# Attention through centers: projections of the next group in pieces, one copy on another engine, the first group in another order, and weight sums pinned later

## The chip, the cores and the metric

The kernel runs on one core of a Trainium2 chip. The metric is device time in microseconds, lower is better: 3571.76 us is the median of three runs before the change (3570.47 to 3575.51). The engines are called as in the profile: PE (TensorE matmul) and PEld (its weight loads), DVE (VectorE), ACT (ScalarE), POOL (GpSimd) and SP (SyncE, which issues most DMAs).

## What is computed

A decoder of four layers; each has an attention part, a cross-attention part and a feed-forward part, each added to `x` (16 sequences of 128 tokens, 256 wide, float32). The part that changes is the attention of layer 1, with 16 heads of width 16 and 64 centers for each head:

```python
def _affinity(t, centers, inv_two_sig2, amplitudes):
    t2 = jnp.sum(t * t, axis=-1, keepdims=True)
    c2 = jnp.sum(centers * centers, axis=-1)[None, :, None, :]
    tc = jnp.einsum('bhnd,hkd->bhnk', t, centers)
    d2 = jnp.maximum(t2 + c2 - 2.0 * tc, 0.0)
    return amplitudes[None, :, None, :] * jnp.exp(-d2 * inv_two_sig2[None, :, None, :])
...
q = split_heads(x @ W_q)
kk = split_heads(x @ W_k)
v = split_heads(x @ W_v)
q_aff = _affinity(q, centers, inv_two_sig2, amplitudes)
k_aff = _affinity(kk, centers, inv_two_sig2, amplitudes)
v_agg = jnp.einsum('bhnk,bhnd->bhkd', k_aff, v)
k_sum = jnp.sum(k_aff, axis=2)
num = jnp.einsum('bhnk,bhkd->bhnd', q_aff, v_agg)
den = jnp.einsum('bhnk,bhk->bhn', q_aff, k_sum) + EPS
out = num / den[..., None]
```

The output is projected with `W_o`. The cross-attention of layer 1 follows; its feed-forward part rescales its weights by the mean of their absolute values (`jnp.mean(jnp.abs(w))`), and the sums for that are computed during the cross-attention.

## The kernel before

The tokens are held in four groups (`x[g]`, 4 tiles of 128 tokens each). A scheduler places the recorded instructions on the engines. An instruction recorded with `keep_in_program_order` (the helpers `pinned`, L257, and `pinned_transpose`, L260) keeps its place among the others recorded so; one recorded with `mm` (L168) or `transpose_group` (L185), and all work on DVE, ACT and POOL, is put where the scheduler likes. PSUM has two sets of buffers: `b1`, four of one bank, and `b2`, two of two banks.

`l1_attn` (L843) loads its weights, scales the centers by the inverse widths, and makes two things of `c2`, the scaled squared lengths of the centers: `c2b` (in rows, for the keys) and `nc2` (through `c2col`, in a column, for the queries).

- `prologue(g)` (L891) is all of a group's projections at once: layernorm, the transposed rows `hT` (PE `tr`, one half copied out by DVE and the other by ACT, `evac`, L108), then `kT` and its squares, `qT` and its squares, and `v` of four tiles, copied by DVE and ACT in turn, beside two POOL memsets each.
- `queries(s, p)` (L916) makes the affinities `qa` of two tiles: 32 small products `yq`, eight exponentials on ACT (L935), and a clamp at 1 by two POOL instructions (L939).
- `keys(s, t)` (L942) does so for the keys of one tile: `yk`, two exponentials `ka` (L968), and the clamp on DVE (L969). A `yk` or a `yq` takes both `b2` buffers.
- `combine(...)` (L972) is a generator in six steps: `agg` and its scaling `vs` (DVE, L982); the transposes `aggT` and their copy `va` (ACT, L988); `num` and its copies `oT` (ACT, L1001); `o16t` and the division (DVE, `normalize`); `ctr` and its copy `cT` (DVE, L1013); the output projection `proj`, added to `x` (L222).

The loop at L1029 runs over the 16 tiles `n` and three iterations more. An iteration makes the keys of tile `n`, begins tile `n-1`, and takes steps of the tiles before. Odd iterations also make the queries of the next two tiles. At the end of the third iteration of each group stands the whole `prologue` of the next.

`xattn64` (L1047) is the cross-attention. It calls `beside[m]` at the end of its unit `m`; for layer 1 these come from `l1_ffn_begin` (L1225). Its `absolute(i)` (L1239) at units 10, 11 and 12 sums a weight matrix: one reduction over 2048 columns (L1241) and one over 16 (L1244), neither pinned.

Of the kernel before, what the change touches and what calls it, by code (L numbers as in the profile page):

```python
# [9 lines left out]
F = mybir.dt.float32  # L10
BF = mybir.dt.bfloat16
U32 = mybir.dt.uint32
AF = mybir.ActivationFunctionType
ALU = mybir.AluOpType
AX = mybir.AxisListType
PSUM = bass.MemoryType.PSUM

P = 128
# [4 lines left out]
NG = 4  # L23
GB = B // NG
GT = GB * P
# [5 lines left out]
class Decoder:  # L31
# [811 lines left out]
    def l1_attn(self):  # L843
# [6 lines left out]
        nc = self.nc  # L850
        wq, wk_, wv, wo = self.load4(["L1_attn_W_q", "L1_attn_W_k", "L1_attn_W_v", "L1_attn_W_o"])
# [5 lines left out]
        S = lambda t: slice(t * P, (t + 1) * P)  # L857
        R = lambda j: slice(32 * j, 32 * j + 32)
        with self.tc.tile_pool(name="l1a", bufs=1) as wk:
            c2b = wk.tile([P, 2, 4, P], F, tag="c2b", name="c2b")  # L860
            nc2 = wk.tile([P, 8], F, tag="nc2", name="nc2")
# [11 lines left out]
            c2 = self.hp.tile([P, 1024], F, tag="h", name="c2", bufs=2)  # L873
# [1 line left out]
            nc.vector.tensor_tensor(c2, cbf, cbf, ALU.mult)  # L875
            nc.vector.tensor_tensor(c2, c2, obf, ALU.mult)
            nc.vector.scalar_tensor_tensor(cbf, cbf, -2.0, obf, ALU.mult, ALU.mult)
            for half in range(2):
                ps = self.b1("c2b")
                self.mm(ps, [(self.ones, c2[:, half * 512 : (half + 1) * 512])])  # L880
                self.evac(c2b[:, half].rearrange("p r n -> p (r n)"), ps)
            ps = self.b1("c2col")[:, 0:8]
            for i in range(8):
                self.mm(ps[:, i : i + 1], [(c2[:, i * P : (i + 1) * P], self.ones[:, 0:1])])
            nc.vector.tensor_scalar(nc2, ps, -1.0, None, ALU.mult)

            for half in range(2):
                v = ob[:, half, :].rearrange("p (h k) -> p h k", h=8)
                nc.vector.tensor_tensor(v, v, self.hmask.unsqueeze(2).to_broadcast([P, 8, 64]), ALU.mult)

            def prologue(g):  # L891
                hT = self.hidden_T(self.layernorm(g))
                res = []
                for name, w in (("kT", wk_), ("qT", wq)):
                    if name == "kT":
                        dst, d2 = (wk.tile([P, 2, GT], F, tag=n, name=n, bufs=2) for n in ("kT", "kT2"))
                    else:
                        dst, d2 = (self.hp.tile([P, 2, GT], F, tag="hT", name=n, bufs=5) for n in ("qT", "qT2"))
                    for half in range(2):
                        ps = self.b1(name)  # L900
                        self.mm(ps, [(w[:, k, half * P : (half + 1) * P], hT[:, k, :]) for k in range(2)])
                        nc.vector.tensor_copy(dst[:, half, :], ps)
                        nc.scalar.activation(d2[:, half, :], dst[:, half, :], AF.Square)
                    res += [dst, d2]
                v = []
                for t in range(GB):
                    vt = wk.tile([P, 16, 32], F, tag="v32", name="v32", bufs=6)
                    nc.gpsimd.memset(vt[:, :, 16:32], 0.0)
                    nc.gpsimd.memset(vt[:, :, 16:17], 1.0)
                    ps = self.b1("v")[:, 0:DM]  # L910
                    self.mm(ps, [(hT[:, k, S(t)], wv[:, k, :]) for k in range(2)])
                    self.evac(vt[:, :, 0:16], ps.rearrange("p (h d) -> p h d", h=16))
                    v.append(vt)
                return res, v

            def queries(s, p):  # L916

                qT, qT2 = s[0][2:]
                cols = slice(p * 256, p * 256 + 256)
                tiles = [self.b2("yq").rearrange("p (r h n) -> p r h n", r=2, h=2) for _ in range(2)]  # L920
                for half in range(2):
                    for k, (w, q) in enumerate(((cb, qT), (ob, qT2))):
                        for r in range(4):
                            self.pinned(
                                tiles[r // 2][:, r % 2, half],
                                w[R(r), half, S(r)],
                                q[R(r), half, cols],
                                start=half == 0 and k == 0,
                                stop=half == 1 and k == 1,
                            )  # L930
                qa = wk.tile([P, 8, 256], F, tag="qa", name="qa", bufs=2)
                for r in range(4):
                    for half in range(2):
                        i = 4 * half + r
                        nc.scalar.activation(  # L935
                            qa[:, i, :], tiles[r // 2][:, r % 2, half], AF.Exp, bias=nc2[:, i : i + 1], scale=-1.0
                        )
                for i in range(0, 8, 4):
                    nc.gpsimd.tensor_scalar(qa[:, i : i + 4, :], qa[:, i : i + 4, :], 1.0, None, ALU.min)  # L939
                return qa  # L940

            def keys(s, t):  # L942

                kT, kT2 = s[0][:2]
                tiles = [self.b2("yk").rearrange("p (r n) -> p r n", r=2) for _ in range(2)]
                for r in range(4):
                    o = slice(32 * r, 32 * r + 1)
# [4 lines left out]
                        start=True,  # L952
                        stop=False,
# [18 lines left out]
            def combine(g, t, v, ka, qa):  # L972
# [12 lines left out]
                for m in range(2):  # L985
                    self.pinned_transpose(ps[:, S(m)], vs[:, S(m)])
                va = wk.tile([P, 2, 4, 32], F, tag="va", name="va", bufs=2)
                nc.scalar.copy(va.rearrange("p m j d -> p (m j d)"), ps)  # L988
                yield
                tiles = [self.b1("num")[:, 0:256] for _ in range(2)]  # L990
                cols = slice((t % 2) * P, (t % 2) * P + P)
# [26 lines left out]
                self.add_x(g, t, ps)  # L1018
                yield

            state = {0: prologue(0)}
            qas = {0: queries(state[0], 0)}
            kas, parts = {}, {}

            def part(n):
                if n in parts:
                    next(parts[n])

            for n in range(B + 3):  # L1029
                g, t = divmod(n, GB)  # L1030
                if n < B:
                    kas[n] = keys(state[g], t)
                part(n - 3)
                k = n - 1
                if 0 <= k < B:
                    parts[k] = combine(k // GB, k % GB, state[k // GB][1][k % GB], kas.pop(k), qas[k // 2])
                    part(k)
                if n % 2 and n + 1 < B:
                    qas[(n + 1) // 2] = queries(state[(n + 1) // GB], (n + 1) // 2 % 2)
                part(n - 2)  # L1040
                part(n - 1)
                part(n - 3)
                part(n - 1)
                if t == GB - 2 and g + 1 < NG:
                    state[g + 1] = prologue(g + 1)

    def xattn64(self, H, names, bias, tag, begin=None):  # L1047

# [176 lines left out]
    def l1_ffn_begin(self):  # L1225


        nc = self.nc
# [9 lines left out]

        def absolute(i):  # L1239
            p16 = self.small([P, 16], "p16")  # L1240
            nc.vector.tensor_reduce(  # L1241
                p16, flats[i].rearrange("p (a n) -> p a n", a=16), AX.X, ALU.add, apply_absolute_value=True
            )
            nc.vector.tensor_reduce(part[:, i : i + 1], p16, AX.X, ALU.add)  # L1244

# [1388 lines left out]
```

## Time and profile before

| | |
|---|---|
| median of three runs | 3571.76 us |
| the profiled execution, its own time | 3571.38 us |
| its span, first to last instruction | 3569.7 us |
| mean granted clock of TensorE over the span | 0.965 |
| the stage: last `down` of the part before, on PE | begins 1027.84 us |
| the stage: first product of its own, `c2b` | 1031.30 us |
| the stage: first product of the next part, `kT` at L1076 | 1219.11 us |
| va copies, L988 on ACT, within the stage | 16, mean 395 ns |
| DVE copies of the same shape out of PSUM, L1013 | 16, mean 419 ns |
| queries' clamp, L939 on POOL | 16, mean 2810 ns |
| keys' clamp, half as wide, L969 on DVE | 32, mean 489 ns |

The profile is one execution. A group of instructions is named by line, engine and operation, then what it writes and reads (`num<-qa,va`), its shape and how many there are. In brackets stands how long the engine had been idle before and what released it. In the tables of stretches, a row has the length of the stretch, busy time of PE, PEld, DVE, ACT and POOL with the number of instructions, the clock granted to TensorE as a share of full speed, the share of the DMA engines and their GB/s. The matmuls of the small forms (32 rows or 32 columns of the array) run beside each other, so that their durations overlap.

### The profile page before, as it was taken

How to read it: one execution, taken by the hardware profiler on the slowest of the kernel's cores; microseconds unless marked ns; L12 is line 12 of the kernel's file. 1: busy time of each engine (PE TensorE's matmuls, PEld its weight loads, DVE VectorE, ACT ScalarE, POOL GpSimd, SP SyncE). 2: the span in 40 equal slices, each digit the busy share in tenths (PEclk: the TensorE clock that was granted, in tenths of full speed). 3: DMA queues.
4: the chain of work that ended last, by engine and by line, in shares of the span. 5: the costliest groups of instructions: out<-in, count | busy, mean ns of one | idle time of the engine just before them, and what ended most of it. 6: DMA issues, size and time to landing. Idle time of an engine off the chain costs nothing.

```text
span 3569.7 us, 51436 instructions
## 1 busy us (share of the span) xinstructions
PE 3297.9 (92%) x20930; PEld 1787.4 (50%) x20947; DVE 2106.1 (59%) x4185; ACT 1426.3 (40%) x1924; POOL 424.5 (12%) x605
## 2 busy tenths in 40 slices
PE   7999999999998899998999997388999999999999
PEld 4666555555566566664555565252222222225656
DVE  5556444444544544568777544326999999953440
ACT  2357111111124322238555322024677777783221
POOL 5420000000013211110000210114000000002100
PEclk9999999999999999999999999697999999999989
DMA  2000000000110100010100000564202020000000
GB/s 78 1 23 15 18 18 23 18 18 23 36 38 2 38 1 1 1 43 8 46 1 13 2 1 1 182 201 131 36 12 32 12 32 11 11 1 26 1 8 18
DMA packets 90500, 105.46 MB, mean 30 GB/s; under 512 B 11380, under 2 KB 72694, under 8 KB 90006
## 3 DMA queue, kind: packets, MB, share of 16 engines
q1 hardware_dynamic: 79672, 89.71, 9.7%
q0 software_dynamic: 4224, 6.43, 0.6%
q10 hardware_dynamic: 6368, 6.03, 0.5%
q8 instruction: 165, 2.70, 0.3%
q14 instruction: 71, 0.58, 0.1%
HBM read 85.53 MB, written 16.60 MB: 29 GB/s over the span
## 4 chain that ended last, share of the span: by engine, by line
PE 79%; DVE 10%; ACT 5%; issue 3%; DMA 2%; POOL 1%; SPq 0%; POOLq 0%; ACTq 0%; DVEq 0%
PE acc L2166 7%; PE down L257 6%; PE gate L257 6%; PE up L257 6%; PE proj L257 6%; PE st L2166 5%; PE one L2166 4%; PE qT L168 4%; PE st L257 4%; PE o L257 2%; PE h L257 2%; DVE mx L2312 2%; PE rb L257 2%; PE fc L168 2%; PE pr L168 2%
## 5 line engine op out<-in xcount | busy, mean ns | idle before, releaser
L2312 DVE TENSOR_REDUCE mx<-one 128x1 f32<-128x512 f32 x1024 | 658.3, 686 | 55.6 <-PE one L2166 46.3
L2449 ACT ACTIVATE e<-st 128x1024 f32<-128x1024 f32 x512 | 497.0, 1021 | 207.2 <-PE st L2166 206.1
L803 ACT ACTIVATE gs<-gate,cols 128x512 f32<-128x512 f32 x132 | 90.7, 687 | 551.1 <-PE gate L257 544.1
L2166 PE MATMUL acc<-e,v 128*32 128x512 f32 x2048 | 284.7, 609 | 0.9 <-ACT e L2449 0.9
L817 DVE SCALAR_TENSOR_TENSOR x<-down,w_all,x 128x256 f32<-128x256 f32 x512 | 212.3, 477 | 110.4 <-PE down L257 110.2
L2166 PE MATMUL st<-qp,kp 113*128 113x512 bf16 x1024 | 271.6, 386 | 4.4 <-DMA qp<-shifts 2.1
L257 PE MATMUL down<-expert,gs 128*128 128x256 f32 x1056 | 249.5, 380 | 2.2 <-DVE gs L804 2.2
L257 PE MATMUL gate<-hT,expert 128*128 128x512 f32 x528 | 248.6, 593 | 0.2 <-ACT hT L712 0.2
L257 PE MATMUL up<-hT,expert 128*128 128x512 f32 x528 | 248.2, 593 | 0.0
L257 PEld LDWEIGHTS down<-expert,gs 128*128 128x128 f32 x1056 | 201.0, 190 | 85.2 <-issue 61.4
L804 DVE SCALAR_TENSOR_TENSOR gs<-up,cols,gs 128x512 f32<-128x512 f32 x132 | 98.9, 750 | 228.7 <-PE up L257 227.8
L2166 PE MATMUL one<-kp,qp 16*128 16x512 bf16 x1024 | 210.9, 395 | 3.7 <-DVE mx L2312 2.4
L2166 PEld LDWEIGHTS <-qp 16*128 16x128 bf16 x1024 | 49.0, 91 | 325.8 <-issue 320.5
L257 PEld LDWEIGHTS up<-hT,expert 128*128 128x128 f32 x528 | 100.5, 190 | 126.1 <-issue 126.1
L2166 PEld LDWEIGHTS <-kp 113*128 113x128 bf16 x1024 | 79.0, 98 | 141.5 <-issue 81.3
L1176 ACT COPY rb<-rb 128x512 f32<-128x512 f32 x64 | 37.4, 585 | 257.5 <-PE rb L257 257.5
L1178 DVE TENSOR_TENSOR cT<-o,rb 128x512 f32<-128x512 f32 x64 | 44.2, 691 | 155.3 <-ACT rb L1176 155.3
L257 PEld LDWEIGHTS gate<-hT,expert 128*128 128x128 f32 x528 | 99.8, 190 | 70.1 <-issue 63.4
L168 PE MATMUL qT<-hT,L_xattn_Wq 128*128 128x512 f32 x256 | 114.1, 599 | 6.7 <-DVE hT L112 4.5
L257 PE MATMUL o<-e,v 128*32 128x128 f32 (+1 forms) x2048 | 104.6, 277 | 12.6 <-DVE nm L294 11.8
L1485 DVE SCALAR_TENSOR_TENSOR xs<-xBC,cols,xs 128x508 f32<-128x508 f32 x144 | 106.0, 741 | 12.3 <-ACT xs L1481 9.0
L257 PEld LDWEIGHTS o<-e,v 128*32 128x32 f32 (+1 forms) x2048 | 80.9, 123 | 28.4 <-POOL e L335 12.3
(536 smaller groups left out, 5393.1 us busy)
## 6 DMA issues: line engine op xcount, KB each, us to landing
W<-in_L_ffn_W_dram SPq DMA_DIRECT2D x46, 512.0 KB, 5.2
expert<-in_L_ffn_Wg_dram SPq DMA_DIRECT2D x32, 128.0 KB, 2.2
expert<-in_L_ffn_Wu_dram SPq DMA_DIRECT2D x32, 128.0 KB, 2.6
expert<-in_L_ffn_Wd_dram SPq DMA_DIRECT2D x32, 128.0 KB, 2.5
parts<-parts SPq DMA_DIRECT2D x16, 256.0 KB, 2.5
qp<-parts SPq DMA_DIRECT2D x28, 128.0 KB, 3.8
kp<-parts SPq DMA_DIRECT2D x12, 256.0 KB, 8.5
hs<-zero SPq DMA_DIRECT2D x23, 128.0 KB, 1.8
```

Source lines behind the costliest of these rows:

```text
L168: self.nc.tensor.matmul(out, lhsT, rhs, start=i == 0, stop=i == n - 1 and bias is None)
L257: self.tc.keep_in_program_order(self.nc.tensor.matmul(*a, **k))
L803: nc.scalar.activation(gs, pg, AF.Silu, bias=bg)
L804: nc.vector.scalar_tensor_tensor(gs, pu, bu, gs, ALU.add, ALU.mult)
L817: nc.vector.scalar_tensor_tensor(xt, pd[:, t, :], w_all[:, o : o + 1], xt, ALU.mult, ALU.add)
L1176: nc.scalar.copy(rb, ps)
L1178: nc.vector.tensor_tensor(cT, po, rb, ALU.mult)
L1485: stt = lambda *a: pin(nc.vector.scalar_tensor_tensor(*a))
L2166: self.tc.keep_in_program_order(nc.tensor.matmul(*a, **k))
L2312: nc.vector.tensor_reduce(mx[:, t, kc, i : i + 1], pair[i], AX.X, ALU.max)
L2449: nc.scalar.activation(e[:, 2 * p : 2 * p + 2, :], ps, AF.Exp, scale=1.0 / 16.0)
```

## The change

It has five parts. (a) The `prologue` becomes a generator of four pieces after the layernorm: `hT`; `qT`; `kT`; `v`. All its matmuls and transposes are pinned, and its PSUM copies all go to DVE. The loop takes one piece in each iteration of the group before: `hT` at the end of the first, `qT` in the second, `kT` at the end of the third and `v` in the fourth; `qT` and `v` are recorded after the step `aggT` and before `proj` and `num`. (b) `va` is copied by DVE. (c) In the first group, `queries` run before `c2b`, `kT` and `v`. (d) The clamp of the first `qa` is on DVE (`queries` takes the engine as an argument). (e) The long reduction of `absolute` is pinned. The diff:

```diff
@@ -875,47 +875,68 @@
             nc.vector.tensor_tensor(c2, cbf, cbf, ALU.mult)
             nc.vector.tensor_tensor(c2, c2, obf, ALU.mult)
             nc.vector.scalar_tensor_tensor(cbf, cbf, -2.0, obf, ALU.mult, ALU.mult)
-            for half in range(2):
-                ps = self.b1("c2b")
-                self.mm(ps, [(self.ones, c2[:, half * 512 : (half + 1) * 512])])
-                self.evac(c2b[:, half].rearrange("p r n -> p (r n)"), ps)
-            ps = self.b1("c2col")[:, 0:8]
-            for i in range(8):
-                self.mm(ps[:, i : i + 1], [(c2[:, i * P : (i + 1) * P], self.ones[:, 0:1])])
-            nc.vector.tensor_scalar(nc2, ps, -1.0, None, ALU.mult)
 
             for half in range(2):
                 v = ob[:, half, :].rearrange("p (h k) -> p h k", h=8)
                 nc.vector.tensor_tensor(v, v, self.hmask.unsqueeze(2).to_broadcast([P, 8, 64]), ALU.mult)
 
+            def products(out, pairs):
+                for i, (l, r) in enumerate(pairs):
+                    self.pinned(out, l, r, start=i == 0, stop=i == len(pairs) - 1)
+
+            def center_lengths():
+
+                ps = self.b1("c2col")[:, 0:8]
+                for i in range(8):
+                    products(ps[:, i : i + 1], [(c2[:, i * P : (i + 1) * P], self.ones[:, 0:1])])
+                nc.vector.tensor_scalar(nc2, ps, -1.0, None, ALU.mult)
+
+            def center_rows():
+
+                for half in range(2):
+                    ps = self.b1("c2b")
+                    products(ps, [(self.ones, c2[:, half * 512 : (half + 1) * 512])])
+                    self.evac(c2b[:, half].rearrange("p r n -> p (r n)"), ps)
+
             def prologue(g):
-                hT = self.hidden_T(self.layernorm(g))
-                res = []
-                for name, w in (("kT", wk_), ("qT", wq)):
-                    if name == "kT":
-                        dst, d2 = (wk.tile([P, 2, GT], F, tag=n, name=n, bufs=2) for n in ("kT", "kT2"))
-                    else:
-                        dst, d2 = (self.hp.tile([P, 2, GT], F, tag="hT", name=n, bufs=5) for n in ("qT", "qT2"))
+
+                h = self.layernorm(g)
+                yield
+                hT = self.hp.tile([P, 2, GT], F, tag="hT", name="hT", bufs=5)
+                for k in range(2):
+                    ps = self.b1("tr")
+                    for t in range(GB):
+                        self.pinned_transpose(ps[:, S(t)], h[:, t, S(k)])
+                    nc.vector.tensor_copy(hT[:, k, :], ps)
+                yield
+
+                def projected(name, w, pool, tag, bufs):
+                    full, squares = (pool.tile([P, 2, GT], F, tag=tag or n, name=n, bufs=bufs) for n in (name, name + "2"))
                     for half in range(2):
                         ps = self.b1(name)
-                        self.mm(ps, [(w[:, k, half * P : (half + 1) * P], hT[:, k, :]) for k in range(2)])
-                        nc.vector.tensor_copy(dst[:, half, :], ps)
-                        nc.scalar.activation(d2[:, half, :], dst[:, half, :], AF.Square)
-                    res += [dst, d2]
+                        products(ps, [(w[:, k, S(half)], hT[:, k, :]) for k in range(2)])
+                        nc.vector.tensor_copy(full[:, half, :], ps)
+                        nc.scalar.activation(squares[:, half, :], full[:, half, :], AF.Square)
+                    return full, squares
+
+                q = projected("qT", wq, self.hp, "hT", 5)
+                yield q
+                k = projected("kT", wk_, wk, None, 2)
+                yield
                 v = []
                 for t in range(GB):
                     vt = wk.tile([P, 16, 32], F, tag="v32", name="v32", bufs=6)
                     nc.gpsimd.memset(vt[:, :, 16:32], 0.0)
                     nc.gpsimd.memset(vt[:, :, 16:17], 1.0)
                     ps = self.b1("v")[:, 0:DM]
-                    self.mm(ps, [(hT[:, k, S(t)], wv[:, k, :]) for k in range(2)])
-                    self.evac(vt[:, :, 0:16], ps.rearrange("p (h d) -> p h d", h=16))
+                    products(ps, [(hT[:, k, S(t)], wv[:, k, :]) for k in range(2)])
+                    nc.vector.tensor_copy(vt[:, :, 0:16], ps.rearrange("p (h d) -> p h d", h=16))
                     v.append(vt)
-                return res, v
-
-            def queries(s, p):
-
-                qT, qT2 = s[0][2:]
+                yield k, v
+
+            def queries(s, p, engine):
+
+                qT, qT2 = s
                 cols = slice(p * 256, p * 256 + 256)
                 tiles = [self.b2("yq").rearrange("p (r h n) -> p r h n", r=2, h=2) for _ in range(2)]
                 for half in range(2):
@@ -936,12 +957,12 @@
                             qa[:, i, :], tiles[r // 2][:, r % 2, half], AF.Exp, bias=nc2[:, i : i + 1], scale=-1.0
                         )
                 for i in range(0, 8, 4):
-                    nc.gpsimd.tensor_scalar(qa[:, i : i + 4, :], qa[:, i : i + 4, :], 1.0, None, ALU.min)
+                    engine.tensor_scalar(qa[:, i : i + 4, :], qa[:, i : i + 4, :], 1.0, None, ALU.min)
                 return qa
 
             def keys(s, t):
 
-                kT, kT2 = s[0][:2]
+                kT, kT2 = s
                 tiles = [self.b2("yk").rearrange("p (r n) -> p r n", r=2) for _ in range(2)]
                 for r in range(4):
                     o = slice(32 * r, 32 * r + 1)
@@ -985,7 +1006,7 @@
                 for m in range(2):
                     self.pinned_transpose(ps[:, S(m)], vs[:, S(m)])
                 va = wk.tile([P, 2, 4, 32], F, tag="va", name="va", bufs=2)
-                nc.scalar.copy(va.rearrange("p m j d -> p (m j d)"), ps)
+                nc.vector.tensor_copy(va.rearrange("p m j d -> p (m j d)"), ps)
                 yield
                 tiles = [self.b1("num")[:, 0:256] for _ in range(2)]
                 cols = slice((t % 2) * P, (t % 2) * P + P)
@@ -1018,8 +1039,17 @@
                 self.add_x(g, t, ps)
                 yield
 
-            state = {0: prologue(0)}
-            qas = {0: queries(state[0], 0)}
+
+
+            pieces = prologue(0)
+            next(pieces)
+            next(pieces)
+            qs = {0: next(pieces)}
+            center_lengths()
+            qas = {0: queries(qs[0], 0, nc.vector)}
+            center_rows()
+            next(pieces)
+            ks = {0: next(pieces)}
             kas, parts = {}, {}
 
             def part(n):
@@ -1028,21 +1058,28 @@
 
             for n in range(B + 3):
                 g, t = divmod(n, GB)
+                ahead = g + 1 < NG
+                if ahead and t == 0:
+                    pieces = prologue(g + 1)
+                    next(pieces)
                 if n < B:
-                    kas[n] = keys(state[g], t)
+                    kas[n] = keys(ks[g][0], t)
                 part(n - 3)
                 k = n - 1
                 if 0 <= k < B:
-                    parts[k] = combine(k // GB, k % GB, state[k // GB][1][k % GB], kas.pop(k), qas[k // 2])
+                    parts[k] = combine(k // GB, k % GB, ks[k // GB][1][k % GB], kas.pop(k), qas[k // 2])
                     part(k)
                 if n % 2 and n + 1 < B:
-                    qas[(n + 1) // 2] = queries(state[(n + 1) // GB], (n + 1) // 2 % 2)
+                    qas[(n + 1) // 2] = queries(qs[(n + 1) // GB], (n + 1) // 2 % 2, nc.gpsimd)
                 part(n - 2)
                 part(n - 1)
+                if ahead and t % 2:
+                    res = next(pieces)
+                    (qs if t == 1 else ks)[g + 1] = res
                 part(n - 3)
                 part(n - 1)
-                if t == GB - 2 and g + 1 < NG:
-                    state[g + 1] = prologue(g + 1)
+                if ahead and not t % 2:
+                    next(pieces)
 
     def xattn64(self, H, names, bias, tag, begin=None):
 
@@ -1238,8 +1275,10 @@
 
         def absolute(i):
             p16 = self.small([P, 16], "p16")
-            nc.vector.tensor_reduce(
-                p16, flats[i].rearrange("p (a n) -> p a n", a=16), AX.X, ALU.add, apply_absolute_value=True
+            self.tc.keep_in_program_order(
+                nc.vector.tensor_reduce(
+                    p16, flats[i].rearrange("p (a n) -> p a n", a=16), AX.X, ALU.add, apply_absolute_value=True
+                )
             )
             nc.vector.tensor_reduce(part[:, i : i + 1], p16, AX.X, ALU.add)
 
```

## The prediction

> **What bounds the kernel now.** I read the table of busy time first, then waits, granted clock and order of time in the one stage that the change touches, attention through centers.
>
> ```profile
> span 3569.7 us, 51436 instructions
> PE 3297.9 (92%) x20930; PEld 1787.4 (50%) x20947; DVE 2106.1 (59%) x4185; ACT 1426.3 (40%) x1924; POOL 424.5 (12%) x605
> ```
>
> TensorE (PE) is busy for 92% of the span: an edit gains what it takes out of PE's idle time or gives back in PE's clock, and nothing else. PE reaches the stage at about 1031 us (after the last `down`) and leaves it at 1219 us (first `kT` of the next layer part): 188 us, 5% of the span. PE's waits from 1031 to 1231 us (in total, times, longest):
>
> ```profile
> PE num L257 <- ACT va L988: 12.8, 8, 3.1
> PE aggT L260 <- DVE vs L982: 6.2, 6, 2.7
> PE yk L257 <- ACT qa L935: 2.4, 2, 1.7
> PE qT L168 <- issue: 2.2, 1, 2.2
> PE kT L168 <- DVE hT L112: 1.5, 4, 0.4
> PE ctr L260 <- DVE l1f L1244: 1.3, 1, 1.3
> PE proj L257 <- DVE cT L1013: 0.6, 1, 0.6
> PE yk L257 <- ACT ka L968: 0.3, 1, 0.3
> ```
>
> They add up to 27.3 us, all the idle time there is to win. The reader is to see that `num` waiting for `va` is nearly half. Where it comes from, in order of time in an odd iteration (start, duration):
>
> ```profile
> 1091.91 3.02 ACT L935 ACTIVATE qa<-yq,nc 128x256 f32<-128x256 f32 x8 [1.87 <-PE yq L257]
> 1092.52 0.38 PE L260 MATMUL aggT<-ident,vs 128*128 128x128 f32 x2
> 1092.73 1.03 PE L257 MATMUL proj<-L_attn_W_q,cT 128*128 128x256 f32 x4
> 1094.77 0.42 ACT L988 COPY va<-aggT 128x256 f32<-128x256 f32 x1
> 1095.34 0.79 PE L257 MATMUL num<-qa,va 64*32 64x128 f32 x32 [1.57 <-ACT va L988]
> ```
>
> `aggT` is finished at 1092.9, but its copy `va` stands on ScalarE behind eight exponentials. The second loss is the clock. Stretches of 8 us: PE, PEld, DVE, ACT, POOL busy, then granted clock:
>
> ```profile
> 1052.00:1060.00 8.00, 6.93 (x80) 5.96 (x80) 0.92 (x2) 2.73 (x7) 5.53 (x2) 0.58 0.01 2
> 1060.00:1068.00 8.00, 4.89 (x84) 3.75 (x90) 1.22 (x3) 4.14 (x11) 1.43 (x3) 0.71 0.00 1
> 1068.00:1076.00 8.00, 7.52 (x148) 5.76 (x133) 2.18 (x7) 2.66 (x7) 5.14 (x4) 0.64 0.01 2
> ```
>
> At a mean clock c, busy time b would be shorter by about (1-c)b: 2.9 + 1.4 + 2.7 = 7.0 us here. The same sum over the stage's other 8-us slices gives 1.7 (1036 to 1044), 1.3 (from 1108), 1.6 (1132 to 1148) and 2.5 (1204 to 1220): 14.1 us in all.
>
> **The change, part by part.** The list of instructions by engine shows as many PE instructions as before, other engines' work moved, and outside this stage and the next layer part no change of order. No DMA is added and SP's order is the same. Sum against the profiled run's 3571.4 us (span 3569.7 and 1.7 around it); the three timed runs have a median of 3571.8, so the two agree.
>
> 1. *`va` to VectorE* (16 copies, two DVE instructions at most between `vs` and it). The copy itself gets no faster: L988 takes 395 ns on ACT, the like copy L1013 419 ns on DVE. It now follows `aggT` at once and ends within `proj` (1.03 us). The Trainium skill ("VectorE: DVE Perf Modes", Specifications) says ScalarE sits closer to PSUM, which speaks against the move. By that rule the edit costs 16 x 24 ns = 0.4 us of DVE and gains nothing; by the wait row it frees 12.8 us. The row decides, since the time is in the queue and not in the copy: -12.4, leaving 0.4.
>
> 2. *Projections in pieces.* `tr` (1.1 us of PE), `qT`, `kT`, `v` (3.6 each) no longer run as one 12-us block; one piece goes into each of four iterations, `qT` and `v` between `aggT` and `proj`/`num`, the others at an iteration's end. PE work is unchanged. The wait of `kT` for `hT` goes in groups 1 to 3 (0.44 + 0.35 + 0.35 = -1.1), because a whole iteration now lies between. The same places would also cover `num`, so parts 1 and 2 share the 12.4 and it is counted once. New in DVE's queue: `hT` half (0.69) and two `v` copies (0.42 each) per group from ACT; with `va` about 3.2 us per group of 41 us. From 1075 to 1171 DVE is busy 44.4 of 96 us; it gets to some 52 of 85, not a bound. On ACT the squares of `kT` and a table load (1.28 us) now precede `ka` in the fourth iterations of groups 1 and 2; `yq` waits for `ka` to free its PSUM tiles: 2 x 0.8 = +1.6 (bounds 0 and 2.6). Lateness of copies in DVE's strict order has no row: bounds 0 and 3, I take +1.0, nearest to the 0.2 to 0.6 that `aggT` waits for `vs` today, a few times.
>
> 3. *First group reordered.* Now: c2b, c2col, `tr`, `kT`, `qT`, `v`, `yq`, then `yk` waits 2.4 us for `qa` to empty PSUM. After: `tr`, `qT`, c2col, `yq`, c2b, `kT`, `v`, `yk`. While ACT does `qa` (3.0 us and the 1.28 load), PE has 9 us of c2b, `kT`, `v`: -2.7 (both `yk` rows). Against it: c2b and c2col (3.4 us) no longer cover `hT`, whose two copies (2 x 0.69) stand behind `x` updates ending at 1033.2. `tr` ends at about 1032.6 and `qT` starts at 1034.0: 1.4 in place of 0.35, +1.0. The clamp goes from POOL (2 x 2.8 us) to DVE (2 x 0.86 by twice L969's 0.43); `kT`'s copies queue behind it and the third `v` product waits for a PSUM buffer, +0.7 (bounds 0 and 2).
>
> 4. *Weight sums later.* Today the scheduler puts L1241 into the stage's tail:
>
> ```profile
> 1206.78 2.29 DVE L1241 TENSOR_REDUCE p<-L_ffn_w_gate 128x16 f32<-128x2048 f32 x1 [0.62 <-DMA L_ffn_w_gate<-in_L_ffn_w_gate_dram]
> 1209.78 0.44 PE L260 MATMUL aggT<-ident,vs 128*128 128x128 f32 x2 [2.74 <-DVE vs L982]
> ```
>
> Gone: this 2.7, `ctr` behind the second sum 1.3, and of the 2.2 before `qT` (its `hT` copy behind the third) 1.7: -5.7. The other 3.5 us of `aggT` waits stay. But the sums do not vanish. Pinned, each stands directly before the reciprocal of an iteration of the next part:
>
> ```profile
> 1372.22 0.42 DVE L222 TENSOR_TENSOR x<-x,proj 128x256 f32<-128x256 f32 x1 [0.26 <-PE proj L257]
> 1372.68 1.16 PE L257 MATMUL st<-qT,kT 64*128 64x128 f32 x16
> 1372.82 0.96 DVE L1163 RECIPROCAL r<-d 128x128 f32<-128x128 f32 x1 [0.18 <-PE d L257]
> 1374.80 1.16 PE L257 MATMUL rb<-r,spread 128*128 128x128 f32 x8
> ```
>
> A sum begun at 1372.64 ends at 1374.93, `r` at 1375.9, `rb` starts at 1376.0 and not 1374.80: 1.2; by the same reckoning 1.4 and 1.1 in its neighbours. +3.7 (bounds 0, if the sums find a hole, and 6.9, all of them).
>
> 5. *Clock.* The half clock from 1053 to 1074 begins right after the 2.4-us `yk` wait, which goes, and the 3.1-us `num` wait within it goes too. The Trainium skill ("TensorE: Matmul & The Clock Gate", What's actually happening) says that one idle window of some 3.4 us halves the clock and one busy window restores it. By the rule the loss here is 1.7 us; the rows show three slices below 0.72 with PE busy 19.3 of 24 us, 7.0 us lost, and full clock only once the dense projections come. The rows decide: 7.0 back, 1.3 and 1.6 behind `num` gaps back, 1.5 of the tail's 2.5; the 1.7 at the start stays and I allow 1.4 more for the new 1.4-us gap and for c2col, whose products are one column wide: -10.0. By the rule it would be -4.7.
>
> Sum: -12.4 - 1.1 + 1.6 + 1.0 - 2.7 + 1.0 + 0.7 - 5.7 + 3.7 - 10.0 = **-23.9 us: 3547.5**, 0.67% faster.
>
> **The rivals.**
> - *The clock does not come back* though the gaps close: 1108 to 1116 has only 1.7 us of idle time and still reads 0.79. Against: from 1171 to 1204, row-tiled work with gaps of 1.5 us ran at 1.00. Then -13.9: **3557.5**. Chance 0.15.
> - *VectorE's order becomes the wait.* It takes `va`, `v`, `hT` and a clamp, and a late `vs` or `ka` stops PE, which is in program order for every matmul now. An odd iteration has about 7 us of PE; if each of the eight lost 1.5 us again, half of the gain goes: **3560**. Against: DVE at 61%. Chance 0.10.
> - *More comes back*: no lateness, sums hidden: -31 to -35, **3538**. Chance 0.13.
> - *Slower: the last group at half clock.* Group 3 has no pieces of a next group in it, and dense projections are what ended the slow stretch at 1075. If the clock halves as it begins, its row-tiled work (38 us busy from 1171 to 1219) takes up to 38 us more: 3547.5 + 38 = **3585**. It decides from 24 us of such work on. Against: today it holds 1.00 there through larger gaps. Chance 0.05.
> - *No effect*, since the `num` waits merely move to `yk` or `o16t`: **3571**. Chance 0.05. What is left, 0.52, is the forecast.
>
> **How the numbers follow.** Range 3537 to 3561: unknown costs (about 8 us each way) and the first three rivals; outside it lie the last two and tails. A measurement of this kernel tells 0.2% (7 us) from no change. Faster by more than that: the forecast, the first three rivals less some of their edge, 0.88; within 0.07; slower 0.05.
>
> **What would show it.** `num` waiting for `va` under 1 us in total; no `yk` wait for `qa`; clock near 1.0 from 1050 to 1205, with a dip around 1036; the stage about 160 us long; three waits of `rb` of 1.1 to 1.4 us in the next part behind the sums. It is wrong if DVE's `vs` or `ka` take over `num`'s wait, or the granted clock of the last group falls.

## The result and the profile after

The changed kernel takes 3552.78 us (median of nine runs, 3542.03 to 3560.3), the kernel before 3575.51 us in nine runs beside it (3565.06 to 3590.2). The ratio is 0.9933 with a 95% interval of 0.9911 to 0.9955: 0.67% faster, as forecast. The first lines of the page after:

```profile
span 3551.1 us, 51415 instructions
PE 3291.6 (93%) x20930; PEld 1776.4 (50%) x20947; DVE 2121.4 (60%) x4215; ACT 1416.5 (40%) x1896; POOL 418.6 (12%) x603
```

The spans differ by 18.6 us, the medians by 22.7. Neither is a good measure of a stage that is 5% of the kernel: identical code in front of the stage took 4.5 us longer in this execution (the last single `down` product begins at 1035.5 us, not 1031.1), and identical code behind it 2.3 us longer. So I read two distances inside one trace: from the start of that last `down` product to the first `kT` of the next layer part ("the stage"), and on to the first `wsum` product, behind the weight sums ("with the sums").

| distance, us | before | after | difference |
|---|---|---|---|
| stage | 188.0 | 161.4 | -26.6 |
| first `kT` to `wsum` | 165.9 | 167.2 | +1.3 |
| with the sums | 353.9 | 328.6 | **-25.3** |

The sum of the forecast was -23.9, and -25.3 + 4.5 + 2.3 = -18.5 is, up to rounding, the difference of the spans.

PE's waits after, from 1035 to 1231 us (in total, times, longest):

```profile
PE aggT L260 <- DVE vs L1003: 5.9, 7, 1.7
PE yq L257 <- ACT ka L989: 2.1, 2, 1.0
PE d L257 <- ACT e L1173: 1.6, 2, 0.8
PE qT L257 <- issue: 1.5, 1, 1.5
PE num L257 <- DVE va L1009: 1.2, 2, 0.7
```

`num`, 12.8 us before, is down to 1.2, and the `yk` and `kT` rows are gone. `aggT` waiting for `vs` is now the largest and hardly changed. (`d` belongs to the next layer part, which begins earlier now.) The same odd iteration in order of time:

```profile
1099.24 3.02 ACT L956 ACTIVATE qa<-yq,nc 128x256 f32<-128x256 f32 x8 [1.87 <-PE yq L257]
1099.85 0.38 PE L260 MATMUL aggT<-ident,vs 128*128 128x128 f32 x2
1100.07 3.60 PE L257 MATMUL qT<-hT,L_attn_W_q 128*128 128x512 f32 x8
1100.27 0.42 DVE L1009 COPY va<-aggT 128x256 f32<-128x256 f32 x1
1103.50 1.03 PE L257 MATMUL proj<-L_attn_W_q,cT 128*128 128x256 f32 x4
1104.46 0.67 PE L257 MATMUL num<-qa,va 64*32 64x128 f32 x32
```

No bracket stands behind `num`: the copy ends at 1100.69 us, and the 3.6 us of the `qT` piece would have hidden it on ScalarE too, whose exponentials end at 1102.26. The clock, in slices of 8 us with the columns of before (granted clock third from the end):

```profile
1052.00:1060.00 8.00, 8.00 (x140) 6.44 (x139) 5.83 (x14) 3.40 (x6) 0.40 (x1) 1.00 0.01 2
1060.00:1068.00 8.00, 8.00 (x128) 5.06 (x130) 2.93 (x7) 4.96 (x13) 3.87 (x3) 1.00 0.01 2
1068.00:1076.00 8.00, 5.75 (x74) 2.93 (x64) 3.21 (x7) 1.59 (x4) 2.35 (x3) 0.79 0.01 2
```

0.79 is the only slice of the stage under 1.00. By (1-c)b it loses 1.2 us, where the stage lost 14.1. All half clock in the stage lasted 34.1 us before and lasts 3.4 after, and PE's busy time in it falls from 162.7 to 149.7 us. In the next layer part the sums show as `rb` waits (and twice more like this, 0.9 us each):

```profile
1342.35 2.27 DVE L1279 TENSOR_REDUCE p<-L_ffn_w_gate 128x16 f32<-128x2048 f32 x1
1344.55 0.95 DVE L1200 RECIPROCAL r<-d 128x128 f32<-128x128 f32 x1
1345.55 1.16 PE L257 MATMUL rb<-r,spread 128*128 128x128 f32 x8 [1.15 <-DVE l1f L1283]
```

The row names L1283, a sum of 0.11 us recorded beside it; what really held `rb` is the chain of the long sum and the reciprocal behind it.

### The profile page after: what moved, and what is told of

The parts are those of the page before. It is cut to its first block, busy times and chain, and to the rows that moved or that the text cites. A ratio compares the mean times of both kernels' runs of the same rounds, so it can differ in the third digit from the quotient of the medians.

```text
span 3551.1 us, 51415 instructions
## 1 busy us (share of the span) xinstructions
PE 3291.6 (93%) x20930; PEld 1776.4 (50%) x20947; DVE 2121.4 (60%) x4215; ACT 1416.5 (40%) x1896; POOL 418.6 (12%) x603
## 4 chain that ended last, share of the span: by engine, by line
PE 79%; DVE 10%; ACT 5%; issue 3%; DMA 1%; POOL 1%; POOLq 0%; DVEq 0%; ACTq 0%
PE acc L2205 7%; PE down L257 7%; PE gate L257 6%; PE up L257 6%; PE proj L257 6%; PE st L2205 5%; PE one L2205 4%; PE st L257 4%; PE qT L168 4%; PE h L257 2%; PE o L257 2%; DVE mx L2351 2%; PE rb L257 2%; PE v L1113 2%; PE fc L168 2%
## 5 line engine op out<-in xcount | busy, mean ns | idle before, releaser
L1213 ACT COPY rb<-rb 128x512 f32<-128x512 f32 x64 | 37.5, 585 | 259.7 <-PE rb L257 259.7
```

The source lines that it names most:

```text
L1213: nc.scalar.copy(rb, ps)
```

## The experiments

Distances in us, each from its own trace; ratios to the kernel before, run on the same chip. The ratios tell all kernels but the third row from the kernel before; between the variants of the kernel after, their intervals overlap, and only the distances tell them apart.

| kernel | stage | with the sums | ratio, 95% |
|---|---|---|---|
| before | 188.0 | 353.9 | |
| `va` copied by VectorE, nothing else | 176.5 | 344.1 | 0.9979 [0.9963, 0.9995] |
| new first group, nothing else | 181.3 | 351.5 | 0.9992 [0.9976, 1.0008] |
| after | 161.4 | 328.6 | 0.9933 [0.9911, 0.9955] |
| after, `va` on ScalarE | 160.8 | 328.0 | 0.9932 [0.9908, 0.9955] |
| after, old first group | 166.4 | 333.6 | 0.9937 [0.9917, 0.9957] |
| after, sums free | 167.1 | 333.1 | 0.9939 [0.9917, 0.9962] |
| after, projections in one block | 169.6 | 336.8 | 0.9969 [0.9941, 0.9997] |
| after, sums behind `rb` | 161.1 | 326.5 | 0.9937 [0.9911, 0.9963] |
| after, `vs` first | 157.4 | 324.5 | 0.9934 [0.9908, 0.9961] |
| after, clamps on VectorE | 158.2 | 325.4 | 0.9932 [0.9905, 0.9958] |
| `vs` first, sums behind `rb` | 157.4 | 322.8 | 0.9925 [0.9903, 0.9947] |
| clamps on VectorE, sums behind `rb` | 158.2 | 323.6 | 0.9920 [0.9895, 0.9945] |
| all three | 154.6 | 320.0 | 0.9931 [0.9908, 0.9955] |

### Parts 1 and 2: does the copy's engine or its cover end the wait?

`va` alone, in the kernel before:

```diff
-                nc.scalar.copy(va.rearrange("p m j d -> p (m j d)"), ps)
+                nc.vector.tensor_copy(va.rearrange("p m j d -> p (m j d)"), ps)
```

> The kernel before with one edit: va is copied by VectorE. Stage means TensorE's time from the end of the last down to the first kT of the cross-attention: 187.8 us before, 161.2 us in the changed kernel. Theory (the wait is ScalarE's queue, and the half clock of 1053 to 1074 belongs to the start, where yk waits for qa): num waits for va 1.5 us or less in place of 12.8, the clock dips behind those waits (2.9 us) go, the half clock at the start stays; stage 171 to 175 us. Rival 1 (the pieces, not the copy, are what fills num's wait; on VectorE the copy only stands in another queue): num still waits 10 us or more, stage 184 or more. Rival 2 (the half clock belongs to the 3.1-us num wait): clock over 0.95 from 1052 to 1076, stage 164 to 168.

The stage is 11.5 us shorter: 176.1 us by the expectation's measure, 1 us over its range. Its waits:

```profile
PE aggT L260 <- DVE vs L982: 10.6, 8, 2.3
PE yk L257 <- ACT qa L935: 3.2, 3, 1.7
PE num L257 <- DVE va L988: 2.3, 4, 0.7
```

`num` falls by 10.5, and `aggT` rises from 6.2 to 10.6: with the `num` gap closed, PE comes to the next `aggT` earlier and waits there for `vs`. Part of a wait moves on to the next producer that was never early. The half clock at the start did not stay as expected: half clock lasts 13.7 us in the whole stage (34.1 before), 6.8 of them in the first spell (10.2 before). So closing the `num` gaps brought clock back too, though less than the second rival had it.

Then the same line undone in the kernel after (`nc.scalar.copy` again).

> The changed kernel with va back on ScalarE, all else kept. Theory (in the second and fourth iterations of groups 0 to 2 a projection of 3.6 us now stands between aggT and num and hides the copy wherever it is): num waits return only in the last group, 1.6 us once and small ones elsewhere; stage 162 to 165 us (161.2 in the changed kernel). Rival (the copy's engine is what removed num's waits): num waits 8 us or more in total, stage 169 or more.

```profile
PE aggT L260 <- DVE vs L1003: 5.4, 7, 1.7
PE yq L257 <- ACT ka L989: 2.1, 2, 1.0
PE num L257 <- ACT va L1009: 2.0, 2, 1.6
```

Both expectations were too high: 160.8 us, no longer than after. `num` waits 0.8 more, once 1.6 in the last group, which has no piece to cover it, and `aggT` 0.5 less. So the pieces close the `num` gaps without the copy's move, and with them its engine is worth nothing that these traces show.

Then `va` left on VectorE and the pieces put back into one block, with the generator run through at the third iteration:

```diff
-                if ahead and t == 0:
-                    pieces = prologue(g + 1)
-                    next(pieces)
...
+                if ahead and t == GB - 2:
+                    pieces = prologue(g + 1)
+                    next(pieces)
+                    next(pieces)
+                    qs[g + 1] = next(pieces)
                     next(pieces)
+                    ks[g + 1] = next(pieces)
```

> The changed kernel with the pieces of each next group (hT, qT, kT, v) run as one block at the end of the group's third iteration, where the kernel before has them; the rest kept (va on VectorE, the new first group, pinned sums). Stage as told for the first runs (161.4 us in the changed kernel, 188.0 before, from the last down to the first kT). Theory (with va on VectorE nothing is left for the pieces to fill but small waits): num waits under 3 us, aggT waits longer for vs (1.1 us in even iterations, as in the run with va alone), kT waits for hT 1.1 us again, yq's 2 us for ka go; stage 161 to 165 us. Rival (the place of the pieces is what keeps the stage and its clock together): stage 169 us or more, or a stretch over 8 us at half clock.

The rival came, by both of its signs: 169.6 us, 8.2 longer, and a spell of 10.2 us at half clock:

```profile
1062.00:1070.00 8.00, 6.94 (x151) 5.19 (x144) 1.88 (x5) 5.03 (x14) 3.62 (x4) 0.90 0.02 3
1070.00:1078.00 8.00, 7.25 (x73) 4.49 (x66) 5.42 (x13) 0.97 (x3) 3.31 (x3) 0.50 0.01 2
```

All waits of the stage together are only 1.5 us longer than after's by the PE rows; PE's busy time is 156.4 us, not 149.7. About 3 us of that is clock. Most of the rest is in the `yk` products, which take 30.5 us of PE's time and not 25.5: eight of the sixteen `yk` last 2.1 to 3.4 us, where after has one over 1.9 us. Their weight loads (PEld) wait within them for the exponentials `qa` to empty PSUM, which the PE rows count as busy. First with one block, then after:

```profile
PEld yk L257 <- ACT qa L956: 3.4, 7, 0.9
PEld yk L257 <- ACT qa L956: 0.4, 1, 0.4
```

So the pieces are worth 8.2 us even where hardly a `num` wait is left for them to hide: a piece between `yq` and the next `yk` also gives ScalarE time to empty PSUM. What the pinning of the projections and their copies on VectorE are worth by themselves, and part (d), no run shows: every kernel with the pieces or with the block has them.

### Part 3: the first group

The old order restored in the kernel after:

```diff
+            center_rows()
+            center_lengths()
             next(pieces)
...
             qs = {0: next(pieces)}
-            center_lengths()
-            qas = {0: queries(qs[0], 0, nc.vector)}
-            center_rows()
             next(pieces)
             ks = {0: next(pieces)}
+            qas = {0: queries(qs[0], 0, nc.vector)}
```

> The changed kernel with the first group in the old order (c2b, c2col, hT, qT, kT, v, then yq), the rest kept. Theory (yk's wait for qa starts the half clock): yk waits 2.4 us again and a stretch of some 15 us after it runs at half clock; stage 167 to 171 us (161.2 in the changed kernel). Rival (pieces close the later gaps, so the clock recovers at the next projection): under 4 us at half clock, stage 161 to 165.

166.4 us lies between the two: 5.0 longer. The 2.4-us `yk` wait is back (1.7 and 0.8), the 1.5-us `qT` wait is 0.3, and a spell of 10.2 us of half clock follows the `yk` wait (the theory had some 15). `aggT` waits 0.9 less, so that the waits add up to 0.4 more; the other 4.6 us are PE's busy time, where the clock is.

The other way round, the new first group with one block, `va` on ScalarE and the sums free (the block's products stay pinned and its copies on VectorE):

> The kernel after with its other three parts undone: the next group's projections in one block behind the third iteration, va copied by ScalarE, sums not held in program order; only the new order of the first group is left. Theory (the start's own worth is the key waits, 2.7 us, and about 5 us of half clock at the beginning): stage from the last down product to the first kT of cross-attention 178 to 182 us against 188.0 of the kernel before. Rival (half clock is a matter of the block and of the num waits, so a better start is lost again within the first iterations): 185 us or more, with half clock over some 15 to 20 us in the first three iterations.

181.3 us, in the theory's range. But the whole gain of 6.7 us does not arrive:

```profile
PE num L257 <- ACT va L1009: 12.5, 8, 2.6
...
PE qT L168 <- issue: 4.0, 1, 4.0
```

The first row is of the stage: the `num` waits are as long as before (12.8), and half clock is only put off to about 1066 us by a first `num` wait. The second is of the next layer part: PE gets there earlier and waits 4.0 us, not 2.2, for an `hT` copy behind the third free sum, then runs at half clock. With the sums the gain is 2.4 us, and the ratio can't be told from 1.

### Part 4: the sums

Not held in program order:

```diff
-            self.tc.keep_in_program_order(
-                nc.vector.tensor_reduce(
...
+            nc.vector.tensor_reduce(
+                p16, flats[i].rearrange("p (a n) -> p a n", a=16), AX.X, ALU.add, apply_absolute_value=True
             )
```

> The changed kernel with the three weight sums not pinned. Theory: they go back into the stage's tail; vs waits behind a sum for 2.3 us or more, stage 165 to 168 us (161.2 in the changed kernel); the three waits of rb in the cross-attention (2.9 us) vanish and its first qT waits 2 us again, so that up to the product of the weight sums the kernel is 3 to 5 us longer than the changed one. Rival (a sum costs TensorE the same wherever it stands): within 1 us of the changed kernel up to that product.

Both ranges held: stage 167.1, with the sums 4.5 us longer. `aggT` waits rise to 7.7 (longest 2.1) and `num` waits to 2.7, the longest of each behind the two sums at the end of the stage, and the slice from 1190 to 1198 us is at 0.50. Half of the stage's loss is wait and half PE's busy time. The `rb` waits vanish as expected; the first `qT` waits 1.2 us and not 2.

Held, but recorded behind the unit's `rb` products (the call of the sums is moved down the loop of the next layer part):

```diff
                     cTs[k] = values(state[k // GB][4][units[k][2]], es.pop(k), r)
+                for work in beside.get(f"mid{m}", ()):
+                    work()
...
-            10: [at(absolute, 0)],
-            11: [at(absolute, 1)],
-            12: [at(absolute, 2)],
+            "mid10": [at(absolute, 0)],
+            "mid11": [at(absolute, 1)],
+            "mid12": [at(absolute, 2)],
```

> The changed kernel with each long weight sum recorded behind the unit's rb products, so that it starts after the reciprocal and the copies of that unit. Theory (rb waits for the reciprocal behind a sum, and for nothing else): the three rb waits (2.9 us) go and no wait of 0.5 us takes their place; last down to the product of the weight sums 325 to 327 us (328.6 in the changed kernel). Rival (VectorE has no room for a sum in a unit): nm or proj waits as long, 328 us or more.

The distance is as the theory has it, 326.5, but not all of the waits go: `rb` waits 1.2 us in all instead of 2.9, twice 0.6, where none of 0.5 was to be left. It is the `rb` of the iteration after a sum.

### The largest wait that stays: `aggT` for `vs`

The only half clock of the kernel after begins behind this (POOL, VectorE and PE rows):

```profile
1064.29 5.53 POOL L960 TENSOR_SCALAR qa<-qa 128x1024 f32<-128x1024 f32 x2 [4.11 <-ACT qa L956]
1068.49 1.86 DVE L990 TENSOR_SCALAR ka<-ka 128x512 f32<-128x512 f32 x2 [2.07 <-ACT ka L989]
1070.27 0.40 DVE L1003 TENSOR_TENSOR vs<-agg,am 128x256 f32<-128x256 f32 x1
1070.73 0.44 PE L260 MATMUL aggT<-ident,vs 128*128 128x128 f32 x2 [1.73 <-DVE vs L1003]
```

Two clamps of `ka` take 1.86 us and not 0.86 (the second alone 1.37), while a clamp runs on POOL; `vs` is queued behind them. Two suspects: the order, and POOL. First the order: the `ka` clamps recorded behind `vs`, both held.

```diff
-                    nc.vector.tensor_scalar(o, o, 1.0, None, ALU.min)
                 return ka
...
+                if n < B:
+                    clamp(kas[n])
```

> The changed kernel with the keys' clamp recorded behind vs and both pinned, so that VectorE does vs before the two clamps of the same iteration. Theory (aggT waits because vs stands behind a clamp that waits for ScalarE): aggT waits 1.5 us or less in total (5.9 in the changed kernel); stage 156.5 to 159 us (161.4). Rival (the clamps only move into the way of va, rsum or the next agg): num, o16t or agg wait as much; stage 160 us or more.

```profile
1063.34 0.42 DVE L1007 TENSOR_TENSOR vs<-agg,am 128x256 f32<-128x256 f32 x1 [2.06 <-PE agg L257]
1063.68 1.88 DVE L995 TENSOR_SCALAR ka<-ka 128x512 f32<-128x512 f32 x2
1065.57 0.41 DVE L1013 COPY va<-aggT 128x256 f32<-128x256 f32 x1
1066.03 1.10 PE L257 MATMUL num<-qa,va 64*32 64x128 f32 x32 [1.77 <-DVE va L1013]
```

The stage came as expected, 157.4, and the `aggT` wait falls to 0.2 us. But the slow pair of clamps now stands ahead of `va`, `num` waits 1.77 us, and one slice is at 0.79 as before. The order only chose who waits. Then POOL: all `qa` clamps on VectorE, the order as in the kernel after.

```diff
-                    qas[(n + 1) // 2] = queries(qs[(n + 1) // GB], (n + 1) // 2 % 2, nc.gpsimd)
+                    qas[(n + 1) // 2] = queries(qs[(n + 1) // GB], (n + 1) // 2 % 2, nc.vector)
```

> The changed kernel with every clamp of the queries' affinities on VectorE (1.3 us for two) in place of GpSimd (5.5 us for two). Theory (a keys' clamp on VectorE is drawn out while a clamp of GpSimd runs, 1.4 us in place of 0.43 at 1069 us): L990 keeps to 0.43 us, aggT's longest wait for vs falls from 1.7 to 0.7 us; stage 159 to 161 us (161.4). Rival (VectorE's queue gets too long: 1.3 us more in each odd iteration before the copies of qT and v): num or yq waits more, stage 162 to 166 us.

```profile
1064.31 1.29 DVE L960 TENSOR_SCALAR qa<-qa 128x1024 f32<-128x1024 f32 x2 [1.51 <-ACT qa L956]
1068.57 0.95 DVE L990 TENSOR_SCALAR ka<-ka 128x512 f32<-128x512 f32 x2 [1.77 <-ACT ka L989]
1069.90 0.44 PE L260 MATMUL aggT<-ident,vs 128*128 128x128 f32 x2 [0.82 <-DVE vs L1003]
```

158.2 us, better than expected: the clamps take 0.95, and every slice of the stage is at 1.00. Two clamps of `qa` cost VectorE 1.29 us; POOL needs 5.53 for the same.

### Together

The same edits combined, in three ways.

> The kernel after with vs ahead of the ka clamps (held in order), the POOL clamps left where they are, and the sums behind the rb products. Theory (the POOL clamp stretches the ka clamps, and va now stands behind them): stage 157 to 158, one num wait of about 1.8 and one slice at about 0.8 of the clock as without the sums' new place; last down to wsum 322 to 324.

> The kernel after with all qa clamps on VectorE and the long sums recorded behind the rb products of the same unit. Theory (the two gains are in different stages and add up): stage 157.5 to 159 us with a granted clock of 1.00 in all its slices, no rb wait, last down to first wsum 323 to 325 us against 328.6 of after; median 3 to 6 us under after's when the code around runs the same. Rival (the sums' new place delays VectorE and gives it back): last down to wsum 325 or more.

> As the kernel with the clamps on VectorE and the sums behind the rb products, with the ka clamps also recorded behind vs, all held in order. Theory (with no POOL clamp beside them the ka clamps take 0.43 us each, so that vs goes first at no price for va): stage 154.5 to 157 us, aggT waits under 0.5 and num waits under 1.5 together, last down to wsum 320 to 322.5. Rival (VectorE's own clamps of qa now stand ahead of vs or va, and the wait changes its name): num or yq waits over 3, stage 158 or more.

All three distances came as their theories have them: 322.8, 323.6 and 320.0 us with the sums. Two waits did not: with clamps and sums `rb` still waits twice 0.6 us, where none was expected, and with all edits `num` waits 2.0, 0.5 more than the theory allowed. With all edits `aggT` waits 0.2, and the clock is 1.00 throughout the stage. By the trace that is 8.6 us less than after in the same stretch. The median of this kernel, 3547.91 us, lies 5 us under after's, and the interval of its ratio [0.9908, 0.9955] covers after's, so that the time of the whole kernel does not tell the two apart. Against the kernel before, all three are faster.

## Why the prediction was right

The forecast had most terms right; two were off in opposite directions and cancel in part. That the ratio agrees to the last digit is luck, since code that is the same in both kernels differed by 6.8 us between the two profiles. Measured against it, over the distance with the sums:

| term | forecast | measured, before to after |
|---|---|---|
| `num` | -12.4 | -11.6 (12.8 to 1.2) |
| `kT` for `hT` | -1.1 | -1.5 |
| new `qT` wait | +1.0 | +1.5 |
| `yq` behind `ka` | +1.6 | +2.1 |
| `aggT`: a sum gone, lateness come | -2.7, +1.0 | -0.3 (6.2 to 5.9) |
| `yk` | -2.7 | -2.7 |
| third `v` product | +0.7 | +0.2 |
| `ctr` and `qT` behind sums | -3.0 | -2.9 |
| `rb` | +3.7 | +2.9 |
| clock | -10.0 | -12.9 (14.1 to 1.2) |
| sum | -23.9 | -25.2 |

The measured terms add up to the -25.3 of the trace within 0.1. The clock row is the (1-c)b of 8-us slices; PE's busy time, which holds the clock, falls by 12.8 us over the same distance (323.7 to 310.9).

- **`va` and pieces** (steps 1 and 2). That the two share one gain was right, and the runs show how: `va` alone ends 10.5 us of `num` waits but pays 4.4 of them back at `aggT`; with the pieces in place, it adds nothing. The step "the row decides, since the time is in the queue" was right about the queue. It credited the gain to the edit that was not needed.
- **Lateness on VectorE**, +1.0 within bounds of 0 and 3, was too small: `aggT` keeps 2.4 us more than the 3.5 that were to stay. About 1 us of it is the one pair of clamps at 1068 us; with POOL's clamps gone, `aggT` drops by 1.6 (5.9 to 4.3). The forecast took the clamp's usual duration and did not ask what runs on POOL meanwhile.
- **The first group** was right in each wait. Its 5.0 us in the full kernel are 1.2 in its own waits, less the 0.9 at `aggT`, and mostly clock. As the only part it gains 2.4, since the `num` waits and the third sum take the rest.
- **The sums**: right, with `rb` 0.8 too high, as the second and third wait are 0.9 and not 1.4 and 1.1.
- **The clock**, -10.0, was 2.9 too small. The dip foreseen at 1036 us did not come: after the 1.5-us wait and the one-column `c2col` the slices read 1.00. One came at 1072 us, behind an `aggT` wait that was not foreseen, and was short.
- **Rivals.** "VectorE's order becomes the wait" showed in part: `aggT` waits seven times for `vs`, 1.7 us at most, but not half of the gain. The last group held 1.00, though in the kernel with free sums its end did fall to 0.50, behind a 2.1-us wait.

The forecast's reading of the slow stretch, "full clock only once the dense projections come", was wrong in detail. The full clock came back at 1063.5 us among row-tiled products, after 10.2 us, and the next `num` gap took it away again at 1066.9. The traces allow a closer reading. In all 14 of them, from 1025 to 1240 us, the clock is either 0.50 or 1.00 and changes only at fixed steps of 3.41 us; a spell of half clock lasts one, two or three of them (3.41, 6.83, 10.24). Four such steps before, then two after, in the columns of the slices above:

```profile
1053.29:1056.69 3.40, 2.93 (x36) 2.56 (x36) 0.01 (x1) 0.77 (x3) 3.40 (x2) 0.50 0.02 5
1056.69:1060.11 3.42, 3.41 (x44) 3.16 (x48) 0.90 (x2) 0.79 (x2) 1.98 (x1) 0.50 0.00 0
1060.11:1063.52 3.41, 3.41 (x57) 2.87 (x60) 1.22 (x3) 0.75 (x2) 0.47 (x2) 0.50 0.01 2
1063.53:1066.93 3.40, 1.09 (x18) 0.50 (x10) 0.00 (x0) 2.63 (x8) 0.00 (x0) 1.00 0.00 0
1068.94:1072.36 3.42, 1.17 (x36) 0.68 (x35) 2.79 (x6) 0.00 (x1) 1.41 (x3) 1.00 0.00 0
1072.37:1075.77 3.40, 3.40 (x4) 1.39 (x5) 0.00 (x0) 0.65 (x2) 0.00 (x0) 0.50 0.02 5
```

PE is busy for all of the second and of the third step, yet half clock follows the one and full clock the other. What separates them is the work in the array. Count for a product its columns, times the share of the 128x128 array that it uses: a `kT` product (128*128, 512 columns) counts 512, a `num` product (64*32, 128 columns) 16.

| kernel, step begins at | clock in it | PE busy | array work | clock in the next |
|---|---|---|---|---|
| before, 1053.3 | 0.50 | 0.86 | 1032 | 0.50 |
| before, 1056.7 | 0.50 | 1.00 | 1049 | 0.50 |
| before, 1060.1 | 0.50 | 1.00 | 1853 | 1.00 |
| before, 1063.5 | 1.00 | 0.32 | 954 | 0.50 |
| after, 1068.9 | 1.00 | 0.34 | 823 | 0.50 |
| after, 1072.4 | 0.50 | 1.00 | 1917 | 1.00 |
| one block, 1065.0 | 1.00 | 0.69 | 1132 | 0.50 |
| clamps on VectorE, 1069.0 | 1.00 | 0.61 | 1680 | 1.00 |

So it is in the 882 steps of the 14 traces between 1025 and 1240 us. Whatever the clock in a step, each of the 40 that were followed by half clock had at most 1519 of array work, and each of the 842 others at least 1508; a border at 1515 puts all but two right. This was counted in traces already taken; no run was made to test it.

That is the second thing the pieces do. The `kT` piece (1072.3 to 1077.7) does 1917 in its first step even at half clock, so that the spell lasts one step; with `vs` first the spell is one step again, under the `kT` piece. Where row-tiled work follows instead, it lasts three: 1053.3 to 1063.5 before, 1050.3 to 1060.5 with the old first group, 1068.4 to 1078.6 with one block. The Trainium skill ("TensorE: Matmul & The Clock Gate", What's actually happening) gives one busy window of about 3.4 us for the return to full clock. The 3.41 us behind `kT` agree; in the other three cases it took three steps, with PE busy in most of them, so a busy PE was not enough there.

## What to carry over

Put a dense independent product into each gap rather than all of them into one block: it hides the wait of the step behind it, it gives the engine that empties PSUM time to do so, and it ends a spell of half clock early. For the clock, count the array work in each 3.4 us of these traces, not the longest gap. When two edits aim at the same wait, count it once and then test each alone, since the one with the obvious mechanism (the copy's engine) was worth nothing beside the other. Closing a wait brings the next producer to light: before moving work to VectorE, look at what stands in its queue and at what runs on POOL in the same microsecond.

## What was not expected of the hardware

- A VectorE clamp of `ka` is drawn out beside a POOL clamp of `qa`. In the 14 traces 339 ran without one, the longest in 0.60 us; of 109 beside one, 59 took at most 0.54 us and 50 took 0.63 to 1.54. All of these 50 end at one of four distances from the end of a POOL clamp: 2.6 or 1.45 us ahead of it, 0.28 or 0.53 us behind it, as if they had waited for POOL. That is in line with the exclusive port pair that the Trainium skill describes ("SBUF — State Buffer", SBUF: two separate sides) for some VectorE instructions; but it has the pair held for a whole instruction, and the clamps that end 1.45 us ahead of POOL's end, or run beside it in 0.43 us, do not fit. What is held, and for how long, stays open.
- Half clock needs no long gap: with one block it set in at 1068.4 us behind two waits of 0.52 and 0.54 us, while the kernel with the clamps on VectorE had waits of 0.82 and 0.52 us in a similar place and stayed at 1.00. By length of wait or by PE's busy share the two come out the wrong way round; by array work (1132 and 1680) they do not.
- Whole times differ by more than most of the edits here are worth. The profiled spans of the kernels with all three edits and with the clamps and sums alone are 3530.6 and 3545.0 us, their medians 3547.91 and 3547.66. Of the 14.4 us between the two spans 3.6 lie in the distance with the sums, 8.5 in front of it and 2.3 behind it. The code in front is the same in all 14 kernels, and its length goes with the half clock in it: the last `down` begins at 1027.9 and 1028.1 us with 13.7 us of half clock, at 1030.4 to 1031.1 with 17.1, at 1035.5 to 1036.6 with 30.7, and at 1038.4 with 34.1 and 37.5. Why that differs from run to run is not shown.
